# Two-layer graph network: the attention-weighted sum of a layer-1 tile is kept in a PSUM bank instead of SBUF

## The chip, the core and the metric

The kernel runs on one core of a Trainium2 chip. The metric is device time in microseconds of one execution. Engines are named as the profile names them: PE is TensorE, DVE is VectorE, ACT is ScalarE, POOL is GpSimd, SP is SyncE. SBUF is the large on-chip memory, PSUM the small one[...], into which TensorE writes.

## The reference

The input is a matrix `x` of 3327 nodes by 512 features and a symmetric 0/1 adjacency matrix `adj` with about eight ones to a row. Layer 0 is a four-headed graph attention, layer 1 the gated layer that the change touches; each is added to its input and normalised. Layer 1 on the normalised `x` of layer 0 is:

```python
type_sum_a = adj_a @ x                       # adj_a = adj_b = adj
type_sum_b = adj_b @ x
attn_a = sigmoid(concatenate([type_sum_a, x], axis=1) @ Wa.T + ba)
attn_b = sigmoid(concatenate([type_sum_b, x], axis=1) @ Wb.T + bb)
h = x @ W_sa
scores = (h @ a_sa[0, :Hd])[:, None] + (h @ a_sa[0, Hd:])[None, :]
e = where(adj_a != 0, exp(-leaky_relu(scores, 0.01)), 0.0)
attn = e / (sum(e, axis=1, keepdims=True) + 1e-05)
x_a = attn @ h
x_b = adj_b @ (x @ W_gcnb) + b_gcnb
out = sigmoid(attn_a * x_a + attn_b * x_b)
x = layernorm(x + out)
```

## The kernel before

The kernel never multiplies by the adjacency matrix. A first stage (to about 165 us) reads it and makes, for each node, a list of its neighbours; nodes are sorted by degree and cut into 26 tiles of 128, so that all nodes of a tile have about the same number of neighbours. `CAPS[j]` is the number of neighbours that tile `j` provides for (14 down to 4, 226 over all tiles). Two tiles (`T0`, tiles 0 and 12) hold the nodes of highest degree; neighbours above 14 are packed into one extra set of rows, the "stairs", and TensorE, with the 0/1 matrix `to_node`, brings them back to their nodes.

A gather is one indirect DMA, issued by POOL (L650), that fetches for each of a tile's 128 nodes the row of one neighbour into a slot of a ring of 42 slots in SBUF. Layer 0 uses some 250 of these, layer 1 228. In layer 1, which the change touches, the sums over neighbours are taken before the weight matrices: `attn @ (x W) = (attn @ x) W`.

For each tile layer 1 makes two sums over the gathered rows:

- the weighted sum `sw`, on DVE. `scaled_first` (L1030) has ACT write the node's own row times its weight (L1033). Then `weighted` (L1040) adds one neighbour after another with one `scalar_tensor_tensor` each (L1049): gathered row times a weight of one number per partition, plus `sw`, back into `sw`. For a tile of `T0`, PE multiplies the scaled stairs by `to_node` into a bank of its own, `stair_sum` (L1038), and a last `tensor_add` on DVE (L1053) adds that to `sw`.
- the plain sum, on PE, as matmuls with the identity (L1070, `plain_sum`). To spare matmuls, DVE first adds up to four or five pairs of rows in the ring (L1051), so that a pair costs one matmul. This is why L1051 alternates with L1049 and why PE waits for it.

Both sums are then turned (four transposes each, L1080), copied out of PSUM by ACT (L1082) and multiplied by `W_sa` and `W_gcnb` into one bank (`project`, L1089); DVE adds the bias (L1119), ACT takes the tanh (L1121), DVE adds the row (L1143) and takes the statistics of the norm (L725). Once in up to four tiles ACT normalises the finished tiles (L1136) and POOL scatters them.

There is no scheduler here: the order of work on every engine is that of the statements. Iteration `i` of the last loop interleaves three tiles: it turns and projects tile `i-1`, sums tile `i` in two parts (`weighted(j, 0)` with the pairs, `weighted(j, 1)` with the rest), computes the weights of tile `i+1` (`weights_a`, `weights_b`) and seeds its sum (`scaled_first(j1)`), and finishes tile `i-2`. So on DVE the last addition of tile `i` stands ahead of the weights of tile `i+1` (L1014), and these stand ahead of the seed on ACT, for which the first addition of tile `i+1` waits. `sw` has two buffers, `stair_sum` one.

Of the kernel before, what the change touches and what calls it, by code (L numbers as in the profile page):

```python
# [8 lines left out]
F32 = mybir.dt.float32  # L9
AF = mybir.ActivationFunctionType  # L10
ALU = mybir.AluOpType
# [3 lines left out]
P = 128  # L15
# [10 lines left out]
CAPS = (14, 12, 11, 10, 9, 9, 8, 8, 7, 6, 6, 5) + (14, 13, 11, 10, 10, 9, 9, 8, 8, 7, 7, 6, 5, 4)  # L26
# [52 lines left out]
def sparse_pass(  # L79
# [39 lines left out]
    nc = tc.nc  # L119
    N, F = out.shape  # L120
# [8 lines left out]
    T0 = (0, NG[0])  # L129
# [38 lines left out]
    to_node = const.tile([P, P], F32, name="to_node")  # L168
# [5 lines left out]
    def place(j):  # L174

        return (0, j) if j < NG[0] else (1, j - NG[0])
# [5 lines left out]
    def row1(j):  # L182
        g, i = place(j)
        return x1[g][:, i, :]
# [459 lines left out]
    got, stair = {}, {}  # L644
# [260 lines left out]
    for i in range(NT + 3):  # L905
# [10 lines left out]
        if 0 < i <= NT:  # L916
            j = order0[i - 1]
# [7 lines left out]
            if done:  # L925
                k0, scale, shift = done
# [25 lines left out]
    m1 = ctx.enter_context(tc.tile_pool(name="m1", bufs=2))  # L952
    ps1 = ctx.enter_context(tc.tile_pool(name="ps1", bufs=1, space=PSUM, side="right"))
# [12 lines left out]
        order += long[:1] + short[:1]  # L966
        short, long = short[1:], long[1:]
    order += last
    ew, gates, sums, plain, proj, zs, stair_sum = {}, {}, {}, {}, {}, {}, {}

    def own_score(j):
        ew[j] = m1.tile([P, S + 1], F32, tag="e", name=f"e{j}", bufs=3)
# [46 lines left out]
    def paired(j):  # L1019

        left = 4 + (CAPS[j] >= 13)
        got_ = set()
        for s0, n, g, _ in got[j]:
            for i in range(0, n - 1, 2):
                if left:
                    got_.add(s0 + i)
                    left -= 1
        return got_

    def scaled_first(j):  # L1030

        sw = sums[j] = m1.tile([P, F], F32, tag="sw", name=f"sw{j}")
        nc.scalar.activation(sw, row1(j)[:, 0:F], AF.Copy, scale=ew[j][:, 0:1])  # L1033
        if j in T0:
            scaled = m1.tile([P, F], F32, tag="scaled", name=f"scaled{j}", bufs=1)
            nc.scalar.activation(scaled, stair[j][:, 0:F], AF.Copy, scale=ws2[j])
            stair_sum[j] = ps1.tile([P, F], F32, tag="stair", name=f"stair_sum{j}")
            nc.tensor.matmul(stair_sum[j], to_node, scaled, start=True, stop=True)  # L1038

    def weighted(j, part):  # L1040

        e, sw, two = ew[j], sums[j], paired(j)
        cut = max(two) + 2
        for s0, n, g, _ in got[j]:
            for i in range(n):
                s = s0 + i
                if (s < cut) != (part == 0):
                    continue
                nc.vector.scalar_tensor_tensor(sw, g[:, i, 0:F], e[:, s : s + 1], sw, ALU.mult, ALU.add)  # L1049
                if s - 1 in two:  # L1050
                    nc.vector.tensor_add(g[:, i, 0:F], g[:, i - 1, 0:F], g[:, i, 0:F])  # L1051
        if part == 1 and j in T0:
            nc.vector.tensor_add(sw, stair_sum[j], sw)  # L1053

    def plain_sum(j, sums_of_two):
        two = paired(j)
# [41 lines left out]
    weights_a(at_(0))  # L1098
    weights_b(at_(0))
    scaled_first(at_(0))  # L1100
    ready = None
    for i in range(NT + 3):
        j, j1, jp, jpp = at_(i), at_(i + 1), at_(i - 1), at_(i - 2)
# [10 lines left out]
        if j is not None:  # L1114
            plain_sum(j, False)
            weighted(j, 0)
# [11 lines left out]
        if j is not None:  # L1128
            weighted(j, 1)
        if jp is not None:  # L1130
            project(jp, 1)
        if ready:
            k0, scale, shift = ready
# [10 lines left out]
        if j1 is not None:  # L1144
            weights_b(j1)
            scaled_first(j1)
# [382 lines left out]
def gat_then_gated_gnn(tc, x, xT, xB, xL, adj, adjT, adjB, adjL, diag, xo, W0, W0B, b0, a_self, a_neigh, *rest):  # L1529
    N = adj.shape[0]  # L1530
    with tc.tile_pool(name="flag", bufs=1) as pool:
        flag = pool.tile([1, 1], I32, name="flag")
        sparse_pass(tc, flag, x, xB, xL, adjB, adjL, diag, xo, W0B, b0, a_self, a_neigh, *rest)
        with tc.If(tc.nc.values_load(flag[0:1, 0:1]) > 0):
            dense_pass(tc, x[:N], xT, adj, adjT, W0, b0, a_self, a_neigh, *rest)
# [65 lines left out]
```

## Time and profile before

| what | value |
|---|---|
| median of 3 runs | 1110.31 us (1102.92 to 1116.70) |
| the profiled execution | 945.74 us |
| its span, first to last instruction | 943.7 us |
| layer 1: first gather to the last instruction | 549 to 943.7 us |
| PE / DVE / ACT / POOL busy over the span | 783.3 / 733.8 / 275.7 / 607.1 us |
| mean granted TensorE clock | 0.913 of full speed |

The profiled execution is 164.6 us shorter than the median of the timed runs. In a row of instruction groups the entries are: line, engine, operation, output from inputs with their sizes, number of instructions, then busy time in us and the mean of one in ns, then the idle time of the engine ahead of them and what ended it. In a timeline, each line is start, duration, engine, line and operation. A row of a table by stretches gives the length and then for each engine its busy time and instruction count, the granted clock, the share of DMA time and the rate.

### The profile page before, as it was taken

What the parts mean: (1) busy time and instruction counts of PE and PEld (TensorE: products, weight loads), DVE (VectorE), ACT (ScalarE), POOL (GpSimd) and SP (SyncE); (2) the same over time, 40 slices, a digit from 0 to 9 for tenths busy, and PEclk for the clock granted to TensorE, in tenths of its full rate; (3) what the DMA queues carried; (4) which work ended last, traced back from release to release, by engine and by line L of the source; (5) the groups of instructions that cost most, each with busy time, mean ns of one, the idle gap of its engine ahead of it and who ended that gap; (6) DMA issues with size and microseconds to landing.
All of it is one profiled execution on the core that took longest, in us unless ns stands there. A gap on an engine that the chain in (4) does not pass through costs nothing. (4 is left out here: it accounts for less than half of the span.)

```text
span 943.7 us, 10295 instructions
## 1 busy us (share of the span) xinstructions
PE 783.3 (83%) x2516; PEld 409.0 (43%) x2516; DVE 733.8 (78%) x2095; ACT 275.7 (29%) x793; POOL 607.1 (64%) x654
## 2 busy tenths in 40 slices
PE   4698976338999697998886939999999999999893
PEld 3377764113555343444443514444444444444341
DVE  4287887786988588796575838798989989999973
ACT  1122211004345244435152403223223232232231
POOL 6711154777777775677777167777777777777611
PEclk9799997558999988999988858999999999999997
DMA  9999999999778786787777157776667676676501
GB/s 335 367 363 393 392 327 391 385 376 325 205 204 249 223 259 196 254 268 233 214 231 229 52 168 195 199 192 189 196 188 201 182 193 191 190 194 187 173 23 48
DMA packets 71990, 221.44 MB, mean 235 GB/s; under 512 B 12912, under 2 KB 16960, under 8 KB 71024
## 3 DMA queue, kind: packets, MB, share of 16 engines
q0 software_dynamic: 46560, 153.64, 54.4%
q1 hardware_dynamic: 22704, 64.94, 18.2%
q10 hardware_dynamic: 2656, 2.10, 0.7%
q8 instruction: 23, 0.38, 0.2%
q14 instruction: 47, 0.39, 0.1%
HBM read 199.78 MB, written 28.32 MB: 242 GB/s over the span
## 5 line engine op out<-in xcount | busy, mean ns | idle before, releaser
L650 POOL DMA_INDIRECT ring<-table,srt x464 | 476.6, 1027 | 154.4 <-issue 62.2
L835 PE MATMUL acc<-ring,ident 128*128 128x512 f32 x504 | 246.7, 636 | 34.5 <-DVE ring L834 22.5
L1049 DVE SCALAR_TENSOR_TENSOR sw<-ring,e,sw 128x512 f32<-128x512 f32 x226 | 169.5, 750 | 11.7 <-ACT sw L1033 5.6
L835 PEld LDWEIGHTS acc<-ring,ident 128*128 128x128 f32 x504 | 97.0, 201 | 150.2 <-issue 77.9
L1070 PE MATMUL acc<-ring,ident 128*128 128x512 f32 x262 | 126.7, 613 | 20.2 <-DVE ring L1051 10.4
L829 DVE TENSOR_TENSOR ring<-ring,w 128x512 f32<-128x512 f32 x176 | 112.1, 694 | 0.6
L368 PE MATMUL pf<-w,xc 128*128 128x260 f32 x416 | 98.0, 396 | 13.8 <-DVE w L308 13.8
L1089 PE MATMUL po<-wsa,sT 128*128 128x512 f32 x208 | 95.1, 600 | 0.3 <-ACT sT L1082 0.3
L1089 PE MATMUL po<-wg,sT 128*128 128x512 f32 x208 | 94.5, 597 | 0.0
L368 PEld LDWEIGHTS pf<-w,xc 128*128 128x128 f32 x416 | 81.0, 197 | 28.3 <-DVE w L308 14.2
L827 ACT ACTIVATE ring<-ring,w 128x128 f32<-128x128 f32 x304 | 91.6, 390 | 1.0 <-DVE w L810 0.9
L1070 PEld LDWEIGHTS acc<-ring,ident 128*128 128x128 f32 x262 | 49.2, 193 | 90.2 <-issue 45.9
L1051 DVE TENSOR_TENSOR ring<-ring 128x512 f32<-128x512 f32 x95 | 65.7, 692 | 3.3
L378 POOL DMA_DIRECT2D table<-row x26 | 14.4, 552 | 76.6 <-ACT st L377 76.6
L396 PE MATMUL pc<-at,pow 128*32 128x512 bf16 (+1 forms) x182 | 25.8, 418 | 44.1 <-DMA at<-in_adjB 30.0
L1089 PEld LDWEIGHTS po<-wsa,sT 128*128 128x128 f32 x208 | 40.2, 194 | 51.2 <-issue 48.8
L1121 ACT ACTIVATE za<-za 128x512 f32<-128x512 f32 x26 | 16.4, 631 | 155.9 <-DVE za L1119 155.9
L1089 PEld LDWEIGHTS po<-wg,sT 128*128 128x128 f32 x208 | 39.8, 192 | 49.9 <-issue 49.2
L144 POOL DMA_INDIRECT out<-za,srt x26 | 28.0, 1078 | 45.2 <-ACT za L1136 38.5
L795 ACT ACTIVATE w<-w 128x40 f32<-128x40 f32 (+10 forms) x26 | 6.2, 238 | 161.7 <-DVE w L794 161.7
L372 ACT COPY row<-pf 128x512 f32<-128x512 f32 x26 | 15.2, 586 | 91.2 <-issue 45.6
L1082 ACT COPY sT<-pt 128x512 f32<-128x512 f32 x52 | 28.5, 587 | 34.7 <-PE pt L1080 34.3
(252 smaller groups left out, 925.9 us busy)
## 6 DMA issues: line engine op xcount, KB each, us to landing
at<-in_adjB SPq DMA_DIRECT2D x78, 512.0 KB, 12.0
ring<-table,srt POOLq DMA_INDIRECT x464, 3.8
table<-row POOLq DMA_DIRECT2D x26, 260.0 KB, 6.0
xc<-in_xB SPq DMA_DIRECT2D x6, 1024.0 KB, 8.6
own<-in_xo SPq DMA_DIRECT2D x1, 3640.0 KB, 30.9
own<-table SPq DMA_DIRECT2D x1, 3640.0 KB, 52.0
at<-in_adjL SPq DMA_DIRECT2D x13, 256.0 KB, 13.4
table<-x1a SPq DMA_DIRECT2D x12, 260.0 KB, 5.4
```

The lines of the kernel that those rows point to most:

```text
L144: put = nc.gpsimd.indirect_dma_start(out=dst, out_offset=bass.IndirectOffsetOnAxis(ap=rows, axis=0), in_=src, in_offset=None, bounds_check ...
L368: nc.tensor.matmul(pf[:, hh, :HC], xc[:, k, o : o + P], w0[:, k, hh, :], start=(k == 0), stop=(k == KT - 1))
L396: nc.tensor.matmul(pc[32 * c : 32 * c + 32, : nt * P], pow2[:, s, :], loaded[i, m], start=(s == 0), stop=(m + 1 not in ms or s == 3),)
L650: nc.gpsimd.indirect_dma_start(out=out_, out_offset=None, in_=table, in_offset=bass.IndirectOffsetOnAxis(ap=ap, axis=0))
L827: nc.scalar.activation(gv[:, h, :], gv[:, h, :], AF.Copy, scale=w[:, s, h : h + 1])
L829: nc.vector.tensor_tensor(gv, gv, w[:, s, :].rearrange("p (h o) -> p h o", o=1).to_broadcast([P, H, FO]), ALU.mult)
L835: nc.tensor.matmul(acc, ident, row, start=(lean and s == 0), stop=(s == CAPS[j] and j not in T0))
L1049: nc.vector.scalar_tensor_tensor(sw, g[:, i, 0:F], e[:, s : s + 1], sw, ALU.mult, ALU.add)
L1051: nc.vector.tensor_add(g[:, i, 0:F], g[:, i - 1, 0:F], g[:, i, 0:F])
L1070: nc.tensor.matmul(plain[j], to, row, start=(not sums_of_two and i == 0), stop=(sums_of_two and i == len(rows) - 1),)
L1082: nc.scalar.copy(sT, pt)
L1089: nc.tensor.matmul(proj[j], sT[:, k, :], wt[:, k, :], start=(half + k == 0), stop=(half + k == KT))
```

## The change

The weighted sum of a tile lives in one PSUM bank, `so_far`, which takes the place of the bank `stair_sum`; all tiles share it. ACT seeds it with the scaled own row. For a tile of `T0` PE's stairs' matmul writes it first, and DVE then adds the own row with one more `scalar_tensor_tensor`; the ACT scaling of the own row and the final `tensor_add` of these tiles go. Each addition but the last reads the bank and writes the bank. The last of a tile (`s == CAPS[j]`) reads the bank and writes the SBUF tile `sw`, which is allocated there and which the transposes read as before. The pair sums stay as they are.

```diff
     def scaled_first(j):
 
-        sw = sums[j] = m1.tile([P, F], F32, tag="sw", name=f"sw{j}")
-        nc.scalar.activation(sw, row1(j)[:, 0:F], AF.Copy, scale=ew[j][:, 0:1])
+        sw = so_far[j] = ps1.tile([P, F], F32, tag="so_far", name=f"so_far{j}")
         if j in T0:
             scaled = m1.tile([P, F], F32, tag="scaled", name=f"scaled{j}", bufs=1)
             nc.scalar.activation(scaled, stair[j][:, 0:F], AF.Copy, scale=ws2[j])
-            stair_sum[j] = ps1.tile([P, F], F32, tag="stair", name=f"stair_sum{j}")
-            nc.tensor.matmul(stair_sum[j], to_node, scaled, start=True, stop=True)
+            nc.tensor.matmul(sw, to_node, scaled, start=True, stop=True)
+        else:
+            nc.scalar.activation(sw, row1(j)[:, 0:F], AF.Copy, scale=ew[j][:, 0:1])
 
     def weighted(j, part):
 
-        e, sw, two = ew[j], sums[j], paired(j)
+        e, sw, two = ew[j], so_far[j], paired(j)
         cut = max(two) + 2
+        if part == 0 and j in T0:
+            nc.vector.scalar_tensor_tensor(sw, row1(j)[:, 0:F], e[:, 0:1], sw, ALU.mult, ALU.add)
         for s0, n, g, _ in got[j]:
             for i in range(n):
                 s = s0 + i
                 if (s < cut) != (part == 0):
                     continue
-                nc.vector.scalar_tensor_tensor(sw, g[:, i, 0:F], e[:, s : s + 1], sw, ALU.mult, ALU.add)
+                to = sw
+                if s == CAPS[j]:
+                    to = sums[j] = m1.tile([P, F], F32, tag="sw", name=f"sw{j}")
+                nc.vector.scalar_tensor_tensor(to, g[:, i, 0:F], e[:, s : s + 1], sw, ALU.mult, ALU.add)
                 if s - 1 in two:
                     nc.vector.tensor_add(g[:, i, 0:F], g[:, i - 1, 0:F], g[:, i, 0:F])
-        if part == 1 and j in T0:
-            nc.vector.tensor_add(sw, stair_sum[j], sw)
```

More of the change, by code (lines that the diff above doesn't have):

```diff
@@ L968, in sparse_pass @@
     order += last
-    ew, gates, sums, plain, proj, zs, stair_sum = {}, {}, {}, {}, {}, {}, {}
+    ew, gates, sums, plain, proj, zs, so_far = {}, {}, {}, {}, {}, {}, {}
     def own_score(j):
```

## The prediction, made before the result was known

> **What bounds the kernel now.** I read the page first, for the weight of the changed lines, then the busy time by stretches, for what layer 1 is short of.
>
> ```profile
> PE 783.3 (83%) x2516; PEld 409.0 (43%) x2516; DVE 733.8 (78%) x2095; ACT 275.7 (29%) x793; POOL 607.1 (64%) x654
> PE po L1089 10%; PE acc L1070 8%; DMA ring<-table,srt 4%; DVE sw L1049 3%; PE pt L1080 2%; POOL ring L650 1%; POOL out L144 1%; DVE ring L1051 1%; ACT za L1136 1%; DVE za L1119 1%; DMA ring<-table,ids 0%; ACT sw L1033 0%; DVE za L1143 0%; PE stair_sum L1038 0%; DVE e L1014 0%
> L1049 DVE SCALAR_TENSOR_TENSOR sw<-ring,e,sw 128x512 f32<-128x512 f32 x226 | 169.5, 750 | 11.7 <-ACT sw L1033 5.6 <-PE pt L1080 2.1
> ```
>
> The additions are 169.5 us of DVE, yet 3% of the chain that ended last; PE's two lines there are 18%. The stretches show why that is no licence to ignore DVE:
>
> ```profile
> 611.00:886.00 275.00, 262.79 (x715) 121.50 (x713) 254.04 (x570) 78.60 (x190) 214.97 (x198) 0.99 0.69 192
> ```
>
> In the 275 us from 611 to 886 PE is busy 262.8, DVE 254.0. I then listed every idle time of the two over 0.25 us. DVE has seven, 7.0 us together; the other 14 us are gaps of 0.03 to 0.2 us in chains of dependent instructions. PE's idle time, 12.2 us, is mostly DVE's pair sums coming late, as here:
>
> ```profile
> 703.18 1.13 PE L1070 MATMUL acc<-ring,ident 128*128 128x512 f32 x2 [1.05 <-DVE ring L1051]
> ```
>
> So DVE and PE both run at their limit. Time added on DVE in this stretch is added nearly whole; time saved there is worth at most PE's 12 us.
>
> [...] The trace has the pairs:
>
> ```profile
> L1119 DVE SCALAR_TENSOR_TENSOR za<-bias_g,gate,po 128x512 f32<-128x512 f32 x26 | 19.3, 741 | 5.9 <-PE po L1089 5.9
> L1143 DVE SCALAR_TENSOR_TENSOR za<-za,x1b 128x512 f32<-128x512 f32 x14 | 9.6, 686 | 1.4 <-ACT za L1121 1.4
> L920 DVE SCALAR_TENSOR_TENSOR x1b<-acc,ring 128x512 f32<-128x512 f32 x14 | 9.5, 680 | 4.1 <-PE acc L845 2.4 <-PE acc L835 1.7
> L1111 ACT ACTIVATE sp<-acc,gate 128x512 f32<-128x512 f32 x26 | 17.7, 680 | 8.6 <-PE acc L1070 8.6
> L1033 ACT ACTIVATE sw<-x1b,e 128x512 f32<-128x512 f32 x14 | 10.1, 718 | 25.4 <-DVE e L1014 25.4
> ```
>
> [...] 38 ns less from PSUM (L1111 against L1033).[...] with a weight per partition 741 from PSUM (L1119) against 750 from SBUF (L1049), with a constant 680 against 686. Reading PSUM costs DVE nothing; it saves 6 to 9 ns.[...] a gather takes POOL 0.94 us at least and 1.08 in the mean of layer 1, and the longer ones are those that lie across L1049 and L1051.
>
> **The change part by part.**
>
> *The additions read PSUM.* 228 do afterwards: the 226 of before and one more in each `T0` tile. At 9 ns less (750 to 741): -2.1 us of DVE.
>
> *All but the last of a tile write PSUM:* 228 - 26 = 202. No DVE instruction of the trace writes PSUM, so I bound it. Below, by what PSUM is worth to ACT: -38 ns each, -7.7 us.[...] A dependent addition starts 0.03 us after the end of the one ahead (two L1049 in a row take 1.53 us), so a longer write would be met in full.[...] Nothing hides it: DVE has no slack, and each pair sum waits for the additions ahead of it.
>
> *The stairs come first instead of last.* In a `T0` tile DVE's first addition now waits for PE's matmul, which waits for ACT's scaling:
>
> ```profile
> 708.84 0.71 ACT L1033 ACTIVATE sw<-x1a,e 128x512 f32<-128x512 f32 x1
> 709.45 0.71 ACT L1036 ACTIVATE scaled<-ring,w_l 128x512 f32<-128x512 f32 x1
> 709.58 1.54 DVE L1049 SCALAR_TENSOR_TENSOR sw<-ring,e,sw 128x512 f32<-128x512 f32 x2
> 710.21 1.13 PE L1038 MATMUL stair_sum<-scaled,to_node 128*128 128x512 f32 x2 [1.81 <-ACT scaled L1036]
> ```
>
> The ACT seed of the tile (L1033) goes, so scaling and matmul move up by 0.61 us: the matmul ends at 710.21 + 1.13 - 0.61 = 710.73, and DVE, ready at 709.58, waits 1.15 us. In the other tile it ends at 648.10 against 646.99: 1.11 us. Together +2.3 us on DVE. Queued behind the waiting addition is all of that tile's DVE work, its pair sums with it, and PE waits for those. PE has the matmul 0.61 us earlier, twice; I take no gain for it.
>
> *The exchange in these tiles:* an addition (750) for a `tensor_add` (692), twice: +0.1 us.
>
> *The seed writes PSUM* (24 of L1033)[...]. DVE waits for it visibly six times[...]; I take nothing. What hides the rest is the statistics (L725, 0.69 us) that DVE does meanwhile.
>
> *One bank for all tiles.* The seed of tile `i+1` must wait for the last addition of tile `i`. It already waits for L1014 of its own tile, which DVE does after that addition. Cost nothing; without that order it would be up to the 0.72 us of the seed per tile, 18 us.
>
> *The wait for the transposes of two tiles back* moves from the first addition of a tile (22 had two waits, at 21 ns for the extra one) to the last (7 have): -0.3 us. No DMA and no POOL instruction moves past another.
>
> Sum: -2.1 + 3.0 + 2.3 + 0.1 - 0.3 = +3.0 us on DVE, all of it inside the saturated stretch but for the first and last tiles: 945.7 becomes some 948.7 us. The timed median lies 164.6 us above the profiled run, and no view shows where. I carry the 3.0 over unchanged: 1113.3 us. Were those 164.6 us PE's, at a lower clock, DVE would have slack and the 3.0 would shrink towards 0.
>
> **The rivals.**
>
> *One bank, read and written at once.* Each addition streams 512 numbers out of the bank and 512 into it. If the bank gives DVE one access at a time, the second pass comes on top. What one costs is in the trace: a `tensor_tensor` of 1024 columns takes 1220 ns (L301), of 512 columns 692: 528 ns. Times 202: +107 us, on a DVE without slack, for a span of about 1053 us, and 1110 + 107 = 1217. It counts as slower from 22 us, that is 0.11 us an addition, on. For it: no row shows DVE reading and writing one bank. Against: PE adds into `acc` and `po` in place at 0.43 us a pass of 512[...].
>
> *POOL was the brake.* From 549 to 891 POOL never pauses for longer than its 0.30 us between two issues.[...] of the 0.13 us that a gather takes above 0.95, their share is 169.5 of 251.6 us of such instructions (with L1051 65.7 and L1143 16.4), 0.09 us; times 228 some 20 us. If the gathers set the pace, the time is 1113 - 20 = 1093. Against: after 611 DVE waits for gathered rows only 0.33 us, at one place.
>
> *PSUM is quicker for DVE as it is for ACT:* -7.7 in place of +3.0, and 1103 us.
>
> **How the numbers follow.** Forecast as worked, with additions within 0.03 us of 0.75: 0.50.[...] Quicker writes, 1103: 0.10. POOL, 1093: 0.10. The double pass or something of its size, 1217: 0.17, since this form of instruction is in no row. A measurement of this kernel tells about 2% (22 us) from no change. Faster by that, under 1088, needs POOL's case and more (the whole 0.13 us of 228 gathers is 30 us): 0.06. Slower by that, over 1132.5: the double pass[...]: 0.20. Same: 0.74. The range leaves out the double pass and the far end of POOL's case: from just under POOL's 1093[...].
>
> **What would show it.** The additions' row (now L1054) at 0.74 to 0.76 us with a PSUM output, a new wait of about 1.1 us on PE ahead of the first addition of the two `T0` tiles, PE busy unchanged within 2 us in layer 1, gathers nearer to 0.98 us, and the span within 6 us. Wrong it would be made by additions of 0.8 us and more, by gaps between them longer than 0.05 us, or by waits on the seed in every tile.

## The result and the profile after

The changed kernel takes 1155.74 us (median of 4, 1150.19 to 1169.85) against 1111.56 us before (4 runs, 1102.92 to 1116.70): a ratio of 1.0358, 95% interval 1.0301 to 1.0414. The ratio leaves out the run of 1169.85 us, which lies over 1.5% above the fastest, and is not the quotient of the two medians (1.040). Forecast were 1113 us, with a range up to 1132. By the medians it is 44 us slower, where 3 were forecast.

One thing has to be known to read any number here: executions of both kernels come in two kinds, without pauses (before 942 to 957 us) and with pauses of up to some 30 us (before 1103 to 1155 us), and all runs of one comparison were of one kind, so that ratios are sound but times of different comparisons are not to be mixed.

The timed runs above have the pauses, and so has the profiled execution of after (span 1148.1 us). The profiled execution of before, on which the prediction was built, had none. The page of after, with the lines that answer those shown of before:

```profile
PE 822.0 (72%) x2516; PEld 428.7 (37%) x2516; DVE 733.7 (64%) x2095; ACT 274.6 (24%) x791; POOL 586.4 (51%) x654
...
PE 17%; another core or an unknown queue 8%; issue 7%; DVE 6%; ACT 2%; DMA 1%; POOL 1%; DVEq 0%; POOLq 0%
...
L1054 DVE SCALAR_TENSOR_TENSOR so_far<-ring,e,so_far 128x512 f32<-128x512 f32 x200 | 150.5, 752 | 16.2 <-issue 4.7
...
L1085 ACT COPY sT<-pt 128x512 f32<-128x512 f32 x52 | 28.6, 588 | 119.3 <-remote 62.5
L1122 DVE SCALAR_TENSOR_TENSOR za<-bias_g,gate,po 128x512 f32<-128x512 f32 x26 | 19.3, 743 | 58.9 <-remote 47.5
```

The line that starts with PE 17% gives shares of the span in the chain of work that ended last. Before, this line and the row of the copy L1085 (then L1082) were:

```profile
PE 20%; DVE 7%; issue 6%; DMA 5%; POOL 2%; ACT 2%; POOLq 0%; DVEq 0%
L1082 ACT COPY sT<-pt 128x512 f32<-128x512 f32 x52 | 28.5, 587 | 34.7 <-PE pt L1080 34.3
```

DVE is busy 733.7 us, before 733.8: the added time is not in the changed instructions, which last 752 ns against 750. It is idle time, put down to "remote" and to "another core or an unknown queue", on one core that no other works with: the profile writes this where it can match the event that ended a wait with no work. L1122 stood idle 5.9 us in front before, now 58.9; the copy 34.7, now 119.3.

What such a pause looks like, first on DVE (timeline of after; columns: start, duration, engine, line, operation, idle time before it and its releaser):

```profile
906.07 0.76 DVE L1054 SCALAR_TENSOR_TENSOR so_far<-ring,e,so_far 128x512 f32<-128x512 f32 x1 [0.19 <-DVE so_far L1054]
907.46 0.69 DVE L1056 TENSOR_TENSOR ring<-ring 128x512 f32<-128x512 f32 x1 [0.64 <-DVE so_far L1054]
908.07 0.75 DVE L1054 SCALAR_TENSOR_TENSOR so_far<-ring,e,so_far 128x512 f32<-128x512 f32 x1
910.26 0.75 DVE L1054 SCALAR_TENSOR_TENSOR so_far<-ring,e,so_far 128x512 f32<-128x512 f32 x1 [1.44 <-DVE so_far L1054]
...
918.04 0.75 DVE L1054 SCALAR_TENSOR_TENSOR sw<-ring,e,so_far 128x512 f32<-128x512 f32 x1 [1.51 <-DVE so_far L1054]
...
921.47 0.75 DVE L1122 SCALAR_TENSOR_TENSOR za<-bias_g,gate,po 128x512 f32<-128x512 f32 x1 [1.42 <-remote]
```

and on ACT and PE, which are stopped by it for longer:

```profile
905.11 0.68 ACT L1114 ACTIVATE sp<-acc,gate 128x512 f32<-128x512 f32 x1
921.54 1.07 ACT L1085 COPY sT<-pt 128x512 f32<-128x512 f32 x2 [15.75 <-remote]
```

```profile
904.35 0.60 PE L1083 MATMUL pt<-ident,sw 128*128 128x128 f32 x4
...
922.18 4.03 PE L1092 MATMUL po<-wsa,sT 128*128 128x512 f32 x5 [14.82 <-ACT sT L1085]
```

The transposes that L1085 copies ended at 904.95. The copy begins 16.6 us later, and PE, which needs the copy, stands still for 14.8. POOL issues gathers back to back nearly all the while (a burst from 882 to 918).

What ended these waits is in the trace, though in no view: the times at which the semaphores went up, the counters by which one engine tells the others that a piece of work is done. PE's went up at 903.24 and then, on record, only at 921.45, 921.52 and 921.58. L1122 starts 0.02 us after the first of these three and the copy L1085 0.02 us after the second, but the matmuls that L1122 needs had ended at 904.51 and the transposes at 904.95. So this pause is an update of PE's semaphore that comes nearly 17 us late. In each of the five profiles with pauses, 95 to 112 of PE's recorded updates (544 to 558) come more than 1 us behind the end of the PE instruction nearest ahead of them; in the fifteen without, none does but the last two of the program. (With pauses about a sixth of PE's 659 updates are not on record, so single waits may be put down wrongly.) Of these late updates 62 to 78% come within 6 us after the end of a burst of ten or more indirect DMAs of POOL, and such stretches are 11 to 13% of the time. The lateness thus goes with POOL's issuing; by what way, the traces do not show.

Both layers have such pauses, though only layer 1 was changed. Taken apart at the last row sum of layer 0 (DVE, L920) and at the bias addition of each tile of layer 1 (L1119 before, L1122 after). No execution of the kernel before with pauses was profiled; two variants of it that were no slower, explained with the experiments below, stand in for it. Each row is one execution, all in us:

| execution | pauses | start to the last tile of layer 0 | from there to the 2nd tile of layer 1 | 2nd to last tile of layer 1 | rest |
|---|---|---|---|---|---|
| before (e1_before_again) | no | 536.7 | 56.8 | 337.3 | 14.5 |
| after (e1_after_again) | no | 539.0 | 56.5 | 338.2 | 14.6 |
| before, DVE longer (e2_dve_longer) | yes | 659.1 | 100.3 | 358.2 | 14.5 |
| before, memset (e4_before_paced) | yes | 656.5 | 96.1 | 352.7 | 16.8 |
| after | yes | 652.8 | 99.5 | 381.3 | 14.5 |
| after (e2_after_again) | yes | 669.0 | 99.6 | 379.7 | 14.5 |
| after, memset (e4_after_paced) | yes | 657.5 | 99.1 | 390.6 | 16.6 |

So the pauses cost before and after about the same: 114 to 130 us up to the end of layer 0 and 39 to 44 us at the change of layers. In the tiles of layer 1 they cost the kernel before 15 to 21 us (352.7 and 358.2 against 337.3) and the changed one 42 to 52 (379.7 to 390.6 against 338.2). That difference, 21.5 to 37.9 us, is most of the loss. PE is idle 27.2 and 29.0 us of these stretches in the two variants of before and 45.8 to 59.5 us in the changed kernel, and the time covered by PE updates over 1 us late is 43 and 44 us against 55 to 70. The changed kernel waits longer for late updates there. The direct comparison of the two profiled executions, 1148.1 against 943.7, would have put some 160 us down to the change that have nothing to do with it.

### The profile page after: what moved, and what is told of

Its sections match the earlier page's. It is cut to its first block, busy times and chain, and to the rows that moved or that the text cites. A ratio compares the mean times of both kernels' runs of the same rounds, so it can differ in the third digit from the quotient of the medians.

```text
span 1148.1 us, 10276 instructions
## 1 busy us (share of the span) xinstructions
PE 822.0 (72%) x2516; PEld 428.7 (37%) x2516; DVE 733.7 (64%) x2095; ACT 274.6 (24%) x791; POOL 586.4 (51%) x654
## 3 DMA queue, kind: packets, MB, share of 16 engines
q1 hardware_dynamic: 22704, 64.94, 14.8%
## 5 line engine op out<-in xcount | busy, mean ns | idle before, releaser
L650 POOL DMA_INDIRECT ring<-table,srt x464 | 457.3, 986 | 318.1 <-issue 109.7
L835 PE MATMUL acc<-ring,ident 128*128 128x512 f32 x504 | 263.5, 671 | 77.4 <-DVE ring L834 43.2
L835 PEld LDWEIGHTS acc<-ring,ident 128*128 128x128 f32 x504 | 101.7, 212 | 202.8 <-issue 109.5
L1054 DVE SCALAR_TENSOR_TENSOR so_far<-ring,e,so_far 128x512 f32<-128x512 f32 x200 | 150.5, 752 | 16.2 <-issue 4.7
L1092 PE MATMUL po<-wsa,sT 128*128 128x512 f32 x208 | 103.9, 647 | 44.1 <-ACT sT L1085 37.8
L1073 PE MATMUL acc<-ring,ident 128*128 128x512 f32 x262 | 123.5, 607 | 12.3 <-DMA ring<-table,srt 9.5
L368 PE MATMUL pf<-w,xc 128*128 128x260 f32 x416 | 104.3, 414 | 13.4 <-DVE w L308 13.4
L368 PEld LDWEIGHTS pf<-w,xc 128*128 128x128 f32 x416 | 85.2, 208 | 30.1 <-DVE w L308 14.1
L1092 PEld LDWEIGHTS po<-wsa,sT 128*128 128x128 f32 x208 | 43.0, 210 | 102.7 <-issue 60.4
L1073 PEld LDWEIGHTS acc<-ring,ident 128*128 128x128 f32 x262 | 50.6, 195 | 79.1 <-issue 54.4
L1085 ACT COPY sT<-pt 128x512 f32<-128x512 f32 x52 | 28.6, 588 | 119.3 <-remote 62.5
L1122 DVE SCALAR_TENSOR_TENSOR za<-bias_g,gate,po 128x512 f32<-128x512 f32 x26 | 19.3, 743 | 58.9 <-remote 47.5
L1083 PE MATMUL pt<-ident,sp 128*128 128x128 f32 x104 | 17.9, 300 | 43.3 <-ACT sp L1114 41.6
```

The costliest lines, as they stand in the source:

```text
L368: nc.tensor.matmul(pf[:, hh, :HC], xc[:, k, o : o + P], w0[:, k, hh, :], start=(k == 0), stop=(k == KT - 1))
L650: nc.gpsimd.indirect_dma_start(out=out_, out_offset=None, in_=table, in_offset=bass.IndirectOffsetOnAxis(ap=ap, axis=0))
L835: nc.tensor.matmul(acc, ident, row, start=(lean and s == 0), stop=(s == CAPS[j] and j not in T0))
L1054: nc.vector.scalar_tensor_tensor(to, g[:, i, 0:F], e[:, s : s + 1], sw, ALU.mult, ALU.add)
L1073: nc.tensor.matmul(plain[j], to, row, start=(not sums_of_two and i == 0), stop=(sums_of_two and i == len(rows) - 1),)
L1083: nc.tensor.transpose(pt[:, k, :], src[:, k * P : (k + 1) * P], ident)
```

## The experiments

**1. Is it there without pauses, and which part of the change does what?** Both kernels again and two parts of the change (lines left out are marked `...`): `order_only` puts the stairs first but stays in SBUF; `psum_only` keeps the order of before and adds up in a PSUM bank (here one 128x512 float32 tile in PSUM) in the 24 tiles without stairs.

```diff
# order_only, against before
-        nc.scalar.activation(sw, row1(j)[:, 0:F], AF.Copy, scale=ew[j][:, 0:1])
-        if j in T0:
+        if j not in T0:
+            nc.scalar.activation(sw, row1(j)[:, 0:F], AF.Copy, scale=ew[j][:, 0:1])
+        else:
...
+        if part == 0 and j in T0:
+            nc.vector.scalar_tensor_tensor(sw, row1(j)[:, 0:F], e[:, 0:1], stair_sum[j], ALU.mult, ALU.add)
...
-        if part == 1 and j in T0:
-            nc.vector.tensor_add(sw, stair_sum[j], sw)
# psum_only, against before
-        sw = sums[j] = m1.tile([P, F], F32, tag="sw", name=f"sw{j}")
+        if j in T0:
+            sw = so_far[j] = sums[j] = m1.tile([P, F], F32, tag="sw", name=f"sw{j}")
+        else:
+            sw = so_far[j] = ps1.tile([P, F], F32, tag="stair", name=f"so_far{j}")
...
+                to = sw
+                if s == CAPS[j] and j not in T0:
+                    to = sums[j] = m1.tile([P, F], F32, tag="sw", name=f"sw{j}")
```

> The kernel before, unchanged, for a trace that answers to its timed runs. In the profile after, the additions take 752 ns as before and DVE is busy 733.7 us as before, but all engines stand still for 10 to 30 us at a time, at some ten places. Theory A (such pauses belong to every ordinary execution, the 943.7 us span of the trace of before was an exception): span about 1108 us, clock about 0.84, pauses of PE over 1.9 us summing to some 150 us more than in the 943.7 us trace, in both layers. Theory B (the pauses come with the changed kernel): span near 945 us in the profiled execution and no pause over 10 us in layer 1.

> The changed kernel, unchanged, on the same chip. Both theories: ratio to before 1.03 to 1.04 again, span about 1150 us. If the difference was one of chips or hours, the ratio falls to 1.00 to 1.01.

> Only the order of the two tiles with stairs is changed: PE's stairs' sum comes first and DVE adds the own row to it, everything grows in SBUF as before. Theory 'order' (the two tiles that now start with a wait carry the loss): ratio 1.03 to 1.04. Theory 'PSUM' (the bank in the chain carries it, whatever way it acts): ratio 1.00, plus 2.3 us at most.

> Only the 24 tiles without stairs grow in a PSUM bank, the two with stairs are summed as before (in SBUF, stairs last). Theory 'PSUM': ratio 1.03 to 1.04. Theory 'order': ratio 1.00 to 1.005.

Measured, against 948.17 us of before in the same comparison (no pauses):

| kernel | median us | ratio, 95% interval |
|---|---|---|
| before again | 948.54 | 1.0004, 0.9989 to 1.0018 |
| after again | 947.67 | 0.9993, 0.9975 to 1.0012 |
| order_only | 949.53 | 0.9996, 0.9976 to 1.0016 |
| psum_only | 944.88 | 0.9959, 0.9938 to 0.9981 |

All four expectations had counted on pauses, and this comparison had none, so order and PSUM are not told apart by it. What it shows is that without pauses the change costs nothing. The rows of the changed kernel there, by the tile `so_far` (durations in ns: lowest, median, highest; below, the waits in us and how many):

```profile
L1054 DVE SCALAR_TENSOR_TENSOR so_far<-ring,e,so_far x200: 742/755/757, 561.7 to 916.4; 128x512 f32<-128x512 f32 x100
L1054 DVE SCALAR_TENSOR_TENSOR sw<-ring,e,so_far x26: 737/746/749, 567.7 to 917.2; 128x512 f32<-128x512 f32 x26
...
  DVE so_far L1054: 6.2, 8
...
  DVE so_far L1045: 2.3, 2
```

The two waits for the stairs are the 2.3 us of the prediction to the tenth. The seed is waited for eight times, 6.2 us, as with L1033 before (5.6 us, twelve times). The gathers did become shorter. Layer 1's by the groups of instructions of both kernels in this comparison, before first:

```profile
L650 POOL DMA_INDIRECT ring<-table,srt x226 | 243.9, 1079 | 71.1 <-issue 33.2 <-DMA ring<-table,srt 15.2 <-DVE sw L1049 6.7
```

```profile
L650 POOL DMA_INDIRECT ring<-table,srt x226 | 225.0, 996 | 71.1 <-DMA ring<-table,srt 25.0 <-issue 22.3 <-DVE so_far L1054 5.2
```

83 ns each, where the POOL rival had worked out 90. In `order_only`, whose sums stay in SBUF, a gather still takes 1076 ns, so it is the sum in PSUM that the shorter gathers go with, and not the order of the stairs (in `psum_only` they come one in 1.312 us, experiment 4); by what way, the runs do not show.

**2. With pauses: the change again, and is DVE short of time there?** `dve_longer` is the kernel before with one more small DVE instruction behind each of the 226 additions.

```diff
                 nc.vector.scalar_tensor_tensor(sw, g[:, i, 0:F], e[:, s : s + 1], sw, ALU.mult, ALU.add)
+                nc.vector.tensor_scalar(gates[j][:, 3:4], gates[j][:, 2:3], 1.0, None, ALU.mult)
```

> The changed kernel once more, at another time. The first comparison gave 1155.7 against 1111.6 us (ratio 1.036), the second 947.7 against 948.2 us (0.999): two conditions in which the same program takes 1110 and 948 us. Theory 'condition' (the loss exists only where executions have the long pauses): if before takes about 948 us here, the ratio is 0.997 to 1.003; if it takes about 1110 us, 1.03 to 1.04. Theory 'chance' (the pauses fell differently on the two kernels once): at about 1110 us the ratio is anywhere between 0.97 and 1.04.

> The kernel before with one more small DVE instruction (one column, into an unused column) behind each of the 226 additions, to test the step that DVE has no slack. Each costs DVE 0.10 to 0.17 us with its wait, 23 to 38 us in all. Theory 'DVE without slack': the span grows by 0.8 to 1.0 of that, 20 to 36 us (ratio 1.02 to 1.04). Theory 'PE sets the pace, DVE has slack': it grows by less than half, under 15 us (ratio below 1.015).

This comparison had the pauses: before 1136.90 us. The changed kernel took 1164.21, ratio 1.0242 (1.0198 to 1.0286), so the loss repeats, if smaller than the 1.03 to 1.04 expected. `dve_longer` took 1135.97, ratio 0.9971 (0.9941 to 1.0002); the page's busy line:

```profile
PE 816.2 (72%) x2516; PEld 427.6 (38%) x2516; DVE 742.4 (66%) x2321; ACT 275.8 (24%) x793; POOL 603.5 (53%) x654
```

DVE is busy 8.6 us longer (742.4 against 733.8), where 23 to 38 were expected, and even these were not added to its chain of additions. First an addition and a pair sum of the kernel before, then of `dve_longer`:

```profile
699.47 0.75 DVE L1049 SCALAR_TENSOR_TENSOR sw<-ring,e,sw 128x512 f32<-128x512 f32 x1
700.26 0.69 DVE L1051 TENSOR_TENSOR ring<-ring 128x512 f32<-128x512 f32 x1
```

```profile
1045.01 0.75 DVE L1049 SCALAR_TENSOR_TENSOR sw<-ring,e,sw 128x512 f32<-128x512 f32 x1
1045.68 0.15 DVE L1050 TENSOR_SCALAR gate<-gate 128x1 f32<-128x1 f32 x1
1045.80 0.69 DVE L1052 TENSOR_TENSOR ring<-ring 128x512 f32<-128x512 f32 x1
```

The two are 0.79 us apart either way, and so it is over the whole layer: between two additions in a row the median is 0.780 us in both kernels (113 pairs), between an addition and its pair sum 0.786 (95). The small instruction went into the gap behind each addition. The experiment therefore does not tell whether DVE has slack. That the loss is not DVE's own work rests on the profile after: busy 733.7 us, with additions of 752 ns.

**3. Is it the rate of the gathers?** In the stretches with pauses, many starts on DVE lie on a grid of 0.70 us while POOL issues gathers back to back. Here in code that the change doesn't touch (timeline of e2_after_again; the burst of 49 gathers lasts from 165 to 226):

```profile
183.38 0.21 DVE L431 CAST bn<-ent 128x96 int32<-128x96 f32 x1 [1.01 <-DVE ent L71]
184.09 0.21 DVE L432 TENSOR_SCALAR bn<-bn 128x96 int32<-128x96 int32 x1 [0.50 <-issue]
185.49 0.26 DVE L434 TENSOR_TENSOR code<-ent,bn 128x96 f32<-128x96 f32 x1 [1.19 <-DVE bn L432]
186.89 0.21 DVE L438 TENSOR_SCALAR bit<-code 128x96 int32<-128x96 int32 x1 [1.14 <-DVE code L434]
187.59 0.26 DVE L441 TENSOR_TENSOR cand<-bit,bn 128x96 f32<-128x96 f32 x1 [0.49 <-issue]
```

The starts are 0.71, 1.40, 1.40 and 0.70 us apart. My theory: whatever serves the waits has a step of 0.70 us, gathers that come faster than one in two steps (1.40 us) build up a backlog, and the change, by quickening the gathers of layer 1 (one in 1.295 us instead of 1.385, from start to start within bursts), makes that backlog. Rivals: the additions' access of PSUM, and the stairs first. To tell them apart POOL gets a memset of its own ahead of the gathers (the condition is shortened here):

```diff
+    idle = gp.tile([P, 1], F32, name="idle")
     def indirect(out_, table, ap):
+        if paced[0]:                       # after: every 2nd gather of layer 1; before: every gather
+            nc.gpsimd.memset(idle, 0.0)
         nc.gpsimd.indirect_dma_start(
```

> The changed kernel with a POOL instruction of some 0.19 us (a one-column memset of its own) ahead of every second gather of layer 1, so that gathers that follow each other start about 1.39 us apart, as in the kernel before, in place of 1.30. In the slow condition engines wait long whenever POOL issues gathers back to back, and their starts fall on a grid of 0.70 us. Theory 'gather rate' (something that serves two steps of 0.70 us a gather falls behind when gathers come faster than one in 1.4 us[...]): where before takes 1110 to 1140 us this takes as long as before, ratio 0.99 to 1.01, against 1.024 to 1.036 of the change without it. Theory 'PSUM bank' (the loss comes from the bank itself): ratio 1.02 to 1.04 still. Where before takes 948 us: 1.00 to 1.01 by either.

> The kernel before with that POOL instruction ahead of every gather, in both layers: 1.48 us between gathers in layer 0, 1.57 in layer 1. Theory 'gather rate', where before takes 1110 to 1140 us: the pauses shrink in both layers, ratio 0.90 to 0.96. Theory 'PSUM bank', and every theory in which POOL's pace plays no part: ratio 1.00 to 1.03. Where before takes 948 us: slower, 1.03 to 1.06, since POOL never pauses in layer 1 there and 228 x 0.19 = 43 us are added to it.

> The 24 tiles without stairs grow in the bank, the two with stairs as before. Where before took 948 us its ratio was 0.996. Theory 'gather rate': POOL is as fast as in the changed kernel (gathers 1.30 us apart), so where before takes 1110 to 1140 us the ratio is 1.02 to 1.035. Theory 'order' (the waits of the two tiles with stairs are what the slow condition stretches): 0.99 to 1.005.

> Only the stairs come first, all in SBUF; POOL is as slow as before (1.39 us). Theory 'gather rate': where before takes 1110 to 1140 us the ratio is 0.995 to 1.01. Theory 'order': 1.02 to 1.04.

> The changed kernel with the POOL instruction ahead of every second gather of layer 1, once more, since before took 947 us at the last time. Theory 'gather rate': where before takes 1110 to 1140 us, ratio 0.99 to 1.01. Theory 'PSUM bank' or 'order': 1.02 to 1.04. Where before takes 948 us: 1.00 to 1.005.

> The kernel before with the POOL instruction ahead of every gather of both layers, once more. Theory 'gather rate': where before takes 1110 to 1140 us the pauses shrink in both layers, ratio 0.90 to 0.96. Theories in which POOL's pace plays no part: 1.00 to 1.03. Where before takes 948 us: 1.01 as the last time.

| kernel | e3, no pauses (before 946.90) | e4, pauses (before 1116.54) |
|---|---|---|
| after_paced | 950.20: 1.0017 (0.9998 to 1.0036) | 1159.30: 1.0369 (1.0327 to 1.0410) |
| before_paced | 956.36: 1.0092 (1.0066 to 1.0117) | 1119.15: 0.9984 (0.9939 to 1.0029) |
| psum_only | 945.85: 0.9984 (0.9969 to 0.9998) | not run |
| order_only | 949.15: 1.0026 (1.0006 to 1.0046) | not run |

The loss stands at 3.7% with the memset, but this doesn't refute the theory, as the memset did not do what it was put there for. POOL in e4_before_paced:

```profile
879.65 1.18 POOL L656 DMA_INDIRECT ring<-table,srt  x1 [0.19 <-issue]
880.84 0.11 POOL L655 MEMSET idle<- 128x1 f32 x1
881.14 1.15 POOL L656 DMA_INDIRECT ring<-table,srt  x1 [0.19 <-issue]
```

The gap of 0.30 us between two gathers became 0.11 of memset and 0.19 of gap. The gathers come as before: one in 1.299 us in e4_after_paced (1.295 without memsets), one in 1.377 in e4_before_paced (1.385). What I had expected of the rate failed; the two runs are useful all the same as a pair with pauses, profiled on one chip (1124.08 and 1165.54 us, 5 and 6 us above their medians), and show the loss with hardly a difference in what the engines do. Busy time from the second to the last tile of layer 1, e4_before_paced and then e4_after_paced (columns: stretch, its length, busy time and count of PE, PE's loads, DVE, ACT, POOL; granted clock, DMA share, GB/s):

```profile
753.00:1105.00 352.00, 325.27 (x872) 152.37 (x872) 297.40 (x679) 97.53 (x229) 227.72 (x358) 0.97 0.50 145
```

```profile
757.00:1147.00 390.00, 330.52 (x878) 155.44 (x876) 298.30 (x679) 96.13 (x227) 201.64 (x278) 0.93 0.46 133
```

38 us more, DVE busy 0.9 us more, PE 5.3 (at a granted clock of 0.93 against 0.97), ACT less. And in one and the same tile DVE runs without a break in one, and late in the other. First e4_before_paced, then e4_after_paced:

```profile
891.86 1.58 DVE L1055 SCALAR_TENSOR_TENSOR sw<-ring,e,sw 128x512 f32<-128x512 f32 x2
893.47 0.69 DVE L1057 TENSOR_TENSOR ring<-ring 128x512 f32<-128x512 f32 x1
894.08 1.53 DVE L1055 SCALAR_TENSOR_TENSOR sw<-ring,e,sw 128x512 f32<-128x512 f32 x2
```

```profile
911.64 0.69 DVE L1062 TENSOR_TENSOR ring<-ring 128x512 f32<-128x512 f32 x1 [0.64 <-DVE so_far L1060]
912.25 0.75 DVE L1060 SCALAR_TENSOR_TENSOR so_far<-ring,e,so_far 128x512 f32<-128x512 f32 x1
914.44 0.75 DVE L1060 SCALAR_TENSOR_TENSOR so_far<-ring,e,so_far 128x512 f32<-128x512 f32 x1 [1.44 <-issue]
```

In both POOL is in the midst of a burst there: 32 gathers, one in 1.393 us, against 24, one in 1.292. I went through all bursts of ten gathers and more from the second tile of layer 1 on, and counted the additions and pair sums that follow one of their kind on DVE and start over 0.3 us late. e4_before_paced has none in its bursts of 1.346 to 1.444 us a gather. The changed kernel has 4 of 26 in e4_after_paced, all in the burst just named; 4 of 25 and 4 of 26 in the profile after, in bursts of 1.289 and 1.292 us; and 6 of 27 in e2_after_again, in one of 1.296. All lie in bursts of more than 20 gathers faster than 1.30 us. That fits the theory, but so few bursts prove nothing. Against a sharp limit at two steps speak PE's updates: in e4_before_paced five of them come late, by up to 4.6 us, in a burst of 42 indirect DMAs from 960 to 1019 us, one in 1.416 us. And the tile shown is the one after the second tile with stairs: of the 23.1 us that the profile after has over e2_dve_longer from the 2nd to the last tile, 20.8 lie in six tiles, from the interval in which the first tile with stairs is summed to the one after the second's; of e4's 37.9 it is 23.4. But of the 21.5 us that e2_after_again has over the same e2_dve_longer it is 10.3, and as much lies in one tile far behind them. The order is neither excluded nor shown.

**4. A pace that is one.** Two memsets of 128x60 ahead of each layer-1 gather of the changed kernel; then one of 128x200 and one of 128x144 in bf16. `psum_only` beside each. (Only the tile of each memset is shown.)

```diff
-    idle = gp.tile([P, 1], F32, name="idle")
+    idle = gp.tile([P, 60], F32, name="idle")     # pace2: memset twice, in layer 1
+    idle = gp.tile([P, 200], BF16, name="idle")   # e6_after_pace: once
+    idle = gp.tile([P, 144], BF16, name="idle")   # e7_after_same: once
```

> The changed kernel with two memsets of 128x60 (estimated 0.15 us each, between the rows 128x1 at 0.117 and 128x128 at 0.205) on GpSimd ahead of every layer-1 gather: about 0.1 us of it fits the gap that is there, so the time from gather to gather should go from 1.295 to some 1.45 to 1.50 us, above two steps of 0.70 us. Where the kernel before takes some 1110 to 1140 us: the gather-rate theory expects the loss gone, a ratio of 0.98 to 1.01; the theories of PSUM access and of the stairs' order expect it unchanged, 1.02 to 1.04. Where the kernel before takes some 947 us all expect 0.995 to 1.02 and nothing is told apart.

> The kernel before with the additions of the 24 tiles without stairs in PSUM; the two tiles with stairs and the order are as before. Where the kernel before takes some 1110 to 1140 us: gather rate expects 1.02 to 1.035 (its layer-1 gathers should come every 1.30 us), PSUM access expects the same 1.02 to 1.035, the order alone expects 0.995 to 1.005. Where the kernel before takes some 947 us: 0.995 to 0.999, as it measured there already.

> The changed kernel with one memset of 128x200 in bf16 (estimated 0.26 us, from 128x128 at 0.195 and 128x350 at 0.381) on GpSimd ahead of every layer-1 gather: some 0.11 us fits the gap that is there, so a gather every 1.44 us or so instead of 1.295, over two steps of 0.70 us. Where the kernel before takes some 1110 to 1140 us: the gather-rate theory expects a ratio of 0.98 to 1.01; PSUM access and the stairs' order expect 1.02 to 1.05. Where the kernel before takes some 947 us all expect 1.00 to 1.04, since the last gather comes up to 33 us later, and nothing is told apart.

> The kernel before with the additions of the 24 tiles without stairs in PSUM, the two tiles with stairs and the order as before. Where the kernel before takes some 1110 to 1140 us: gather rate and PSUM access both expect 1.02 to 1.035, the order alone 0.995 to 1.005. Where the kernel before takes some 947 us: 0.995 to 0.999, as measured.

> The changed kernel with a memset of 128x144 in bf16 on GpSimd ahead of every layer-1 gather. From the 128x200 one (0.282 us, a gather every 1.439 us) and the rows of 128x128 (0.195) it should take some 0.22 us and bring the gathers to one in 1.38 us, the rate of the kernel before. Where the kernel before takes some 1110 to 1140 us: the gather-rate theory expects the loss gone, 0.99 to 1.01; PSUM access and the stairs' order expect 1.02 to 1.04. Where the kernel before takes some 947 us: all expect 0.998 to 1.005.

> The kernel before with the additions of the 24 tiles without stairs in PSUM, the two tiles with stairs and the order as before. Where the kernel before takes some 1110 to 1140 us: gather rate and PSUM access both expect 1.02 to 1.035, the order alone 0.995 to 1.005. Where the kernel before takes some 947 us: 0.995 to 0.999, as measured.

None of the three comparisons met pauses, so none could decide. What they measured:

| kernel | a layer-1 gather each, us | median us | ratio, 95% interval |
|---|---|---|---|
| e5_after_pace2 | 1.870 | 1065.22 | 1.1255, 1.1228 to 1.1283 |
| e6_after_pace | 1.439 | 964.51 | 1.0150, 1.0100 to 1.0200 |
| e7_after_same | 1.404 | 958.24 | 1.0101, 1.0068 to 1.0134 |
| e5_psum_only | | 946.42 | 0.9981, 0.9965 to 0.9997 |
| e6_psum_only | 1.312 | 946.25 | 0.9971, 0.9953 to 0.9989 |
| e7_psum_only | 1.312 | 946.26 | 0.9986, 0.9972 to 0.9999 |

The two memsets of e5 cost far more than their time; its timeline:

```profile
600.87 1.06 POOL L655 DMA_INDIRECT ring<-table,srt  x1 [0.56 <-PE pt L1088]
601.93 0.37 POOL L654 MEMSET idle<- 128x60 f32 x2
602.86 1.26 POOL L655 DMA_INDIRECT ring<-table,srt  x1 [0.56 <-issue]
```

0.37 us of memsets, and the gap behind them is 0.56 us where behind one memset it was 0.19. I had expected 1.45 to 1.50 us a gather, and at 1.87 the gathers seem to set the pace: 228 times 0.57 us more are some 130 us, and the kernel took 118 longer than before. One wider memset did as worked out (1.439 for an estimate of 1.44), e7's came out at 1.404 for 1.38. At that rate, 0.02 us slower than the gathers of before (at most 4.3 us over 228 of them), the changed kernel took 10.7 us longer than before, where I had expected 0.998 to 1.005. The prediction's argument that POOL is no brake thus holds for the kernel before at its rate, and not by much for a slower one; what the rest of the 10.7 us beyond these 4.3 is due to, the memsets themselves perhaps, was not found out.

**What stays open:** which property of the change makes the waits for late updates in layer 1 longer. It is not the length of its instructions (752 ns against 750) and not DVE's load (733.7 us against 733.8). Gather rate, PSUM access and the stairs' order would be told apart by e7_after_same and `psum_only` in a comparison with pauses, and there was none. Also open is what holds the updates up, and why only in some executions; a chip of the same number gave both kinds (e3 and e4).

**A version that is a little faster,** where there are no pauses, is `psum_only`: 0.9959, 0.9984, 0.9981, 0.9971 and 0.9986 of the kernel before in five comparisons, each with its interval below 1, or 1.3 to 3.9 us. Where it gains is not shown. Up to the bias addition of layer 1's tenth tile it takes 17.0 to 17.1 us in all five, where e1_before_again has 20.3, with a wait of 1.6 us for the rows of the second stairs; but in the first profile of the kernel before it is 17.4, with a wait of 0.3. With pauses `psum_only` was not run.

## Why the prediction was wrong

The forecast of 1113 us and the range to 1132, whose upper end no trace or run supported, were wrong; the time is 1155.74. What the instructions cost was forecast well, with some luck. The step that failed is the one that carried this cost over from an execution without pauses to executions with them. By its steps:

- **Additions that read PSUM** (-9 ns) **and write it:** the first was read off the trace (741 against 750). The second, the +3.0 us of the sum, is 15 ns for each of the 202 and was a guess of mine: no row of before had DVE writing PSUM. Together 756 ns were forecast, 752 measured; to SBUF 741 and 745. So the output in PSUM costs 7 ns over the 745 of the additions that only read it. In all 202 x 2 ns - 26 x 5 ns = +0.3 us instead of +0.9. Right; but that the guess came so near is luck.
- **The stairs first,** +2.3 us on DVE: measured 2.3 us without pauses; in the profile with pauses the same two waits take 5.2. `order_only` costs -0.4 to +2.5 us by its two ratios (0.9996 and 1.0026). `psum_only`, which differs from the changed kernel only in the two tiles with stairs (their order, and their sums in SBUF), is 2.8 us faster (947.67 - 944.88). Right without pauses, and the waits grow with them.
- **The exchange of an addition for a `tensor_add`,** +0.1 us: too small to be seen in any run.
- **The seed in PSUM,** nothing: 691 ns in the median against 718 in the mean before, and its waits 6.2 us (eight) against 5.6 (twelve, of which the prediction counted six). Right.
- **One bank for all tiles,** nothing: the seed is released by L1014 as before (21 of its waits without pauses), no new wait stands ahead of it. Right.
- **The moved wait,** -0.3 us: not to be told from the rest.
- **The sum,** +3.0 us against the profiled execution: without pauses the ratio 0.9993 (0.9975 to 1.0012) is -2.4 to +1.1 us of 948. The sum was 2 us or more too high; what took the cost of the stairs off again, the quicker gathers perhaps, which it counted at nothing, is not shown.
- **"The timed median lies 164.6 us above the profiled run, and no view shows where. I carry the 3.0 over unchanged":** the step that failed. It took the 164.6 us for a constant. They were waits for late semaphore updates, the timed executions being of the kind that has them and the profiled one not, and they do not stay the same when the kernel is changed: in layer 1's tiles they cost 15 to 21 us before and 42 to 52 after. Why the change lengthens them stays open.
- **"DVE has no slack":** not tried. The work that was to load DVE went into its gaps (experiment 2).
- **"What would show it":** without pauses every sign came true: additions of 0.752 us, two waits of 2.3 us together, PE busy 354.1 us in layer 1 against 354.3, gathers of 0.996 us, a span 3.0 us longer (948.3 against 945.3). All these signs speak of the execution without pauses; none could have shown that those with pauses lose 44 us.

**The rivals.** The double pass in one bank (1217) is out by the 752 ns. That POOL's gathers become shorter was right in kind and size (83 of 90 ns); the 90 were an estimate that took the 0.13 us by which a gather took longer in the mean than 0.95 for the doing of DVE's L1049, L1051 and L1143, and gave the additions (L1049) their share by busy time. That the gathers set the pace was wrong at 1.385 us a gather. (L1143, in its working, is busy 9.6 + 8.2 = 17.8 us, not 16.4; the 0.09 us stays.) The quicker writes (1103) are out by the same row. No rival had waits between engines becoming longer. The profile of an execution without pauses gave no sign of it; the gap of 164.6 us did.

The chances were wrong for the same reason: 0.20 for slower hung almost wholly on the additions' length, and nothing on the 15% of the time that no view explained.

## What to carry to other kernels

When the profiled execution is far shorter than the timed ones, here 945.74 against 1110.31 us, the trace may be of another regime, as it was here: the change's cost in it need not be the cost in the timed one (-2.4 to +1.1 us here without pauses, 44 with them), the unexplained part is a term of its own with its own bounds, and the range has to hold it. Ask for each edit not only what its instructions cost but what it does to the rate of the gathers, and to the order of the waits, that the other regime may depend on. Look at the end of a wait in the times of the semaphores when the profile can't name its releaser. And when a cost is added to test a theory, measure first that it arrived: the memset that was to slow the gathers vanished in their gap, two of them, 0.37 us long, slowed each gather by 0.57, and the small DVE instruction vanished in the gap behind the additions.

## What the runs showed of the hardware that was not expected

- Executions with pauses: 95 to 112 updates of PE's semaphore come more than 1 us after the work that they tell of, one by nearly 17 us in the pause shown, and 62 to 78% of these just after a burst of indirect DMAs of POOL; the engines that wait for them stand still. Many waiting DVE instructions start on a grid of 0.70 us (e2_after_again, 183 to 188 us). In an execution without pauses (e1_after_again, 165 to 353 us) 146 indirect DMAs in a row, one in 1.29 us, bring no update of PE that is over 1 us late.
- A DVE `scalar_tensor_tensor` of 512 float32 that reads and writes the same PSUM bank takes 752 ns and from PSUM to SBUF 745 (profile of after), from SBUF to SBUF 750 (profile of before).
- A GpSimd gather follows 0.30 us behind another and 0.19 us behind one memset of 128x1 (e4_after_paced), 0.56 us behind two of 128x60 (e5_after_pace2).
- A DVE `tensor_scalar` of one column (0.15 us) behind each of a chain of additions leaves their distance at 0.780 us (e2_dve_longer).
